# First stage of a graph network kernel: transpositions between the halves of a chunk's matmuls, and receivers' places ahead of the receiver table

## The chip, the cores and the metric

The kernel runs on one core of a Trainium2 chip. The metric is the device time of one execution in microseconds (us). Three runs of the kernel before the change took 4166.1, 4173.35 and 4174.21 us (median 4173.35). The engines are named as the profile names them: PE is TensorE (matmuls; PEld its weight loads), DVE is VectorE, ACT is ScalarE, POOL is GpSimd, SP is the engine that mostly issues transfers.

## What is computed

One layer of message passing on a graph with 12,500 nodes of 64 features and 412,500 edges of 32 features, all float32, receivers sorted. The reference, cut to what matters:

```python
h = jnp.maximum(_layernorm(x, axis=-1), 0.0)
msg_in = jnp.concatenate([h[senders], h[receivers], edge_features], axis=-1)
messages = swish(msg_in @ W1 + b1) @ W2 + b2
att = softmax(swish(msg_in @ Wa1 + ba1) @ Wa2 + ba2, axis=0)     # over all edges
aggregated = segment_sum(messages * att, receivers)
upd = swish(concatenate([h, aggregated], -1) @ Wu1 + bu1) @ Wu2 + bu2
return x + upd
```

Since `msg_in @ W` is a sum of three products, the kernel multiplies the sender and receiver parts once per node instead of once per edge.

## The kernel before, in words

**First stage** (`gnn_kernel`, L145 to L267). The nodes are padded to 12,544, which is 128 partitions times 98 blocks (`NB`). They are worked in eight chunks of 8, 14, 14, 14, 14, 14, 12 and 8 blocks (`sizes`, L155). SP's queue loads the eight chunks of x (L163), then `src_sb`, `base_sb`, `dst_sb` and `base_p` (L165 to L170): the senders' numbers, the first receiver of each group of edges (twice), and the receivers' numbers. ACT's queue loads the weights in two halves (L112, L113). For each chunk:

- `squares` (L193): DVE makes row sums `total` (L198) and subtracts the mean into `xm` (L200); ACT squares that into `sq` (L203).
- `deviation` (L206): DVE sums the squares (L208), ACT takes the root (L209).
- `normal` (L211): DVE takes the reciprocal (L214) and makes `h`, the normalised and rectified features (L216).
- `senders` (L219): PE transposes two blocks at a time into PSUM tiles `pt` of up to eight blocks (L229, two such buffers); ACT copies them to `hT` (L231); PE multiplies with the sender weights into PSUM tiles `pn` of up to four blocks (L236, four buffers); ACT copies each to `ts` (L238, two buffers); SP's queue writes the finished chunk into the senders' table `ts_d` in DRAM (L239).

All of these stand in an order written out by hand: `pin` (`tc.keep_in_program_order`) keeps each engine's instructions in the order of the source. In turn i that order is `deviation(i)`, `senders(i - 1)`, `squares(i + 2)`, `normal(i)` (L245 to L251). So on ACT, a chunk's two `hT` copies and four `ts` copies stand in a row, and on PE its seven transposes and seven products.

After the last chunk comes the receivers' table (L253 to L264): for each chunk PE multiplies the kept `hT` with the receiver weights (L259, the same `pn` buffers), DVE adds the bias into `tr` (L261, two buffers), and ACT's queue writes it to `tr_d` (L263). ACT's queue then writes a zero tail and all of `hT` to DRAM (L265, L266), which the main stage reads back. Then `windows` (L176) makes the receivers' places on DVE: `dloc`, each edge's receiver relative to its group's first one (L178, L182), `bj` (L184) and `far` (L187, L188).

**Main stage** (`one_pass`). The edges are 403 groups of 1024. `load(g)` has POOL issue eight indirect DMAs per group (L382), each fetching 128 rows of 512 B of `ts_d` by the numbers in `src_sb`, into one of eight `gs` buffers; SP's queue loads the edge features `eo` and receivers `db` of four groups at a time (L391, L394) and a 64-row window of `tr_d` (L401); DVE makes a one-hot block in `eo` (L405) and PE multiplies (L409). `begin(g)` adds both on DVE (L414) and takes tanh on ACT (L415); `end(g)` makes messages and logits on DVE (L425 to L436); `by_node` weighs and sums by receiver (L477, L483). A running maximum makes the softmax one pass. The tile framework hands eight semaphores in turn to POOL's gathers, so each gather waits until the one eight before it has landed; the transfers of SP and ACT share eight others in the same way. A last stage divides by the softmax sum and computes the update.

Of the kernel before, what the change touches and what calls it, by code (L numbers as in the profile page):

```python
# [42 lines left out]
F32 = mybir.dt.float32  # L43
I32 = mybir.dt.int32
AF = mybir.ActivationFunctionType
# [6 lines left out]
P = 128  # L52
D = 64
DE = 32
U = 64
C = 2 * U
# [24 lines left out]
def gnn_kernel(ctx: ExitStack, tc: tile.TileContext, n_edges, x, src, dst, dst_row, first, edge,  # L81
               weights, out):
    nc = tc.nc
    NB = x.shape[0] // P
# [3 lines left out]
    CB = 14 if NB % 14 == 0 else 2  # L88
# [5 lines left out]
    ts_d = dram.tile([NP, C], F32, name="ts_d")  # L94
# [11 lines left out]
    w_all = const.tile([P, sum(n for _, n in PARTS)], F32, name="w_all")  # L106
# [2 lines left out]
        part[name] = w_all[:, at:at + n]  # L109
        at += n  # L110
    nh = sum(n for _, n in PARTS[:HALVED])
    nc.scalar.dma_start(w_all[:, :nh], weights[:, :nh])  # L112
    nc.scalar.dma_start(w_all[:, nh:], weights[:, nh:])  # L113
    w_pair = part["pair"].rearrange("p (r n) -> p r n", r=2)
    wu2h = part["wu2h"].rearrange("p (h d) -> p h d", h=2)
    we, bias, wa2, bu2_r, ba2_c = (part[k] for k in ("we", "bias", "wa2", "bu2", "ba2"))
# [36 lines left out]
    with tc.tile_pool(name="node1", bufs=1) as node1, \  # L153
            tc.tile_pool(name="node", bufs=2) as node, \
            tc.tile_pool(name="node_ps", bufs=2, space=PSUM) as node_ps:  # L155
        x_v = x.rearrange("(p b) d -> p b d", b=NB)

        sizes = [8] + [min(CB, NB - 16 - c) for c in range(0, NB - 16, CB)] + [8] if NB > 16 else [NB]
        chunks = [(sum(sizes[:i]), n) for i, n in enumerate(sizes)]
        xcs = []  # L160
        for c, n in chunks:
            xc = node.tile([P, CB, D], F32, name="xc", bufs=min(len(chunks), 8))[:, :n, :]
            nc.sync.dma_start(xc, x_v[:, c:c + n, :])  # L163
            xcs.append(xc)
        nc.sync.dma_start(src_sb, src)  # L165
        nc.sync.dma_start(base_sb[:, :NG], first)
        dst_sb = node1.tile([P, T], I32, name="dst_sb")
        nc.sync.dma_start(dst_sb, dst)
        base_p = node1.tile([P, NG], I32, name="base_p")
        nc.sync.dma_start(base_p, bass.AP(tensor=first.tensor, offset=first.offset,  # L170
                                          ap=[[0, P], [1, NG]]))
        hT = node1.tile([2 * D, NB // 2, P], F32, name="hT")

        pin = tc.keep_in_program_order

        def windows():  # L176

            pin(nc.vector.tensor_tensor(dloc.rearrange("p (g k) -> p g k", k=K),  # L178
                                        dst_sb.rearrange("p (g k) -> p g k", k=K),
                                        base_p[:, :, None].to_broadcast([P, NG, K]), ALU.subtract))  # L180
            last4 = dloc.rearrange("p (g k) -> p g k", k=K)[:, :, H:]
            pin(nc.vector.tensor_scalar(last4, last4, -float(SHIFT), None, op0=ALU.add))  # L182
            for h in range(2):
                pin(nc.vector.tensor_scalar(bj[:, :, h], base_p[:WR, :], iota_p[:WR], float(SHIFT * h),  # L184
                                            op0=ALU.add, op1=ALU.add))
            fall = node1.tile([P, NG - 1], F32, name="fall")
            pin(nc.vector.tensor_tensor(fall, base_p[:, :NG - 1], base_p[:, 1:], ALU.subtract))  # L187
            pin(nc.vector.tensor_reduce(far[:, 2:3], fall, AX.X, ALU.max))  # L188

        eps = node1.tile([P, 1], F32, name="eps")  # L190
        nc.vector.memset(eps, EPS)
        xms, sqs, rstds, hs = {}, {}, {}, {}

        def squares(i):

            n = chunks[i][1]
            total = node.tile([P, CB], F32, name="total")[:, :n]
            pin(nc.vector.tensor_reduce(total, xcs[i], AX.X, ALU.add))  # L198
            xm = xms[i] = node.tile([P, CB, D], F32, name="xm", bufs=3)[:, :n, :]
            pin(nc.vector.scalar_tensor_tensor(xm, total[:, :, None].to_broadcast([P, n, D]), -1.0 / D,  # L200
                                               xcs[i], op0=ALU.mult, op1=ALU.add))
            sq = sqs[i] = node.tile([P, CB, D], F32, name="sq", bufs=3)[:, :n, :]
            pin(nc.scalar.activation(sq, xm, AF.Square))  # L203

        def deviation(i):
            n = chunks[i][1]  # L206
            rstd = rstds[i] = node.tile([P, CB], F32, name="rstd")[:, :n]
            pin(nc.vector.tensor_reduce(rstd, sqs.pop(i), AX.X, ALU.add))  # L208
            pin(nc.scalar.activation(rstd, rstd, AF.Sqrt, bias=eps, scale=1.0 / D))  # L209

        def normal(i):  # L211
            n = chunks[i][1]
            rstd = rstds.pop(i)
            pin(nc.vector.reciprocal(rstd, rstd))  # L214
            h = hs[i] = node.tile([P, CB, D], F32, name="h")[:, :n, :]
            pin(nc.vector.scalar_tensor_tensor(h, xms.pop(i), 0.0,  # L216
                                               rstd[:, :, None].to_broadcast([P, n, D]),
                                               op0=ALU.max, op1=ALU.mult))

        def senders(i):  # L220
            c, nn = chunks[i]
            h = hs.pop(i)
            ts = node.tile([P, CB, C], F32, name="ts")[:, :nn, :]
            pts = []
            for b in range(0, nn, 8):
                n = min(8, nn - b)
                pt = node_ps.tile([P, 4, P], F32, name="pt")
                for k in range(n // 2):
                    pin(nc.tensor.transpose(pt[:, k, :], h[:, b + 2 * k:b + 2 * k + 2, :], ident))  # L229
                q = (c + b) // 2  # L230
                pin(nc.scalar.copy(hT[:, q:q + n // 2, :], pt[:, :n // 2, :]))  # L231
            for b in range(0, nn, 4):
                m = min(4, nn - b)
                pn = node_ps.tile([P, 4, C], F32, name="pn", bufs=4)
                for k in range(0, m, 2):
                    pin(nc.tensor.matmul(pn[:, k:k + 2, :], hT[:, (c + b + k) // 2, :],  # L236
                                         w_pair[:, 0], start=True, stop=True))
                pin(nc.scalar.copy(ts[:, b:b + m, :], pn[:, :m, :]))  # L238
            pin(nc.sync.dma_start(ts_d.rearrange("(p b) f -> p b f", b=NB)[:, c:c + nn, :], ts))  # L239

        squares(0)
        if len(chunks) > 1:
            squares(1)
        pin(nc.vector.tensor_scalar(w_all[:, :nh], w_all[:, :nh], 0.5, None, op0=ALU.mult))
        for i in range(len(chunks)):  # L245
            deviation(i)
            if i:
                senders(i - 1)
            if i + 2 < len(chunks):
                squares(i + 2)  # L250
            normal(i)  # L251
        senders(len(chunks) - 1)
        for c, nn in chunks:  # L253
            tr = node.tile([P, CB, C], F32, name="tr")[:, :nn, :]
            for b in range(0, nn, 4):
                n = min(4, nn - b)
                pn = node_ps.tile([P, 4, C], F32, name="pn", bufs=4)
                for i in range(0, n, 2):
                    pin(nc.tensor.matmul(pn[:, i:i + 2, :], hT[:, (c + b + i) // 2, :],  # L259
                                         w_pair[:, 1], start=True, stop=True))  # L260
                pin(nc.vector.tensor_tensor(tr[:, b:b + n, :], pn[:, :n, :],  # L261
                                            bias[:, None, :].to_broadcast([P, n, C]), ALU.add))
            pin(nc.scalar.dma_start(  # L263
                tr_d[:NP, :].rearrange("(p b) f -> p b f", b=NB)[:, c:c + nn, :], tr))  # L264
        pin(nc.scalar.dma_start(tr_d[NP:, :], zero[:WR, :]))  # L265
        pin(nc.scalar.dma_start(hT_d, hT))  # L266
        windows()  # L267

    one_pass(tc, n_edges, locals())
    again = nc.values_load(wrong[0:1, 0:1], min_val=0, max_val=1,  # L270
# [615 lines left out]
```

## Time and profile before

One execution was profiled.

| what | value |
|---|---|
| median of three runs | 4173.35 us |
| time of the profiled execution | 4166.68 us |
| its span, first to last instruction | 4164.9 us |
| DVE busy | 2873.2 us (69%) |
| POOL busy | 3052.8 us (73%) |
| PE busy | 2237.8 us (54%) |
| ACT busy | 600.9 us (14%) |
| first gather starts | 56.44 us |
| last gather starts | 4091.0 us |
| DVE, ACT busy from 0 to 56.4 us | 34.96, 30.91 us |

A row of the page's fifth part names the source line, the engine and operation, the tile written and the tiles read, shapes and count; then the busy time and the mean ns of one; then the idle time just before such instructions and what ended most of it. "issue" there means that the engine waited for nothing that the profile shows. A row of the timeline gives the start, the duration, the engine, the line and the tiles; in brackets stands the idle time before it and what released it. Equal instructions that follow closely are merged into one row with their count. A float32 product counts as two matmul records. Queues are marked by a q: SPq and ACTq rows are the issuing of transfers, not the transfers.

### The profile page before, as it was taken

Reading aid. Unit: us, or ns where it says so; the run is one execution under the profiler, and the core shown is the slowest. Engines: PE = TensorE matmul, PEld = TensorE weight load, DVE = VectorE, ACT = ScalarE, POOL = GpSimd, SP = SyncE. Lnnn points to the kernel's source line nnn. Section 1 sums busy time; section 2 is a strip of 40 time slices with the busy share of each in tenths; the row PEclk is TensorE's granted clock in tenths of the full one; section 3 lists DMA queues with packets and bytes.
Section 4 is the critical chain, followed back from the end, with each engine's and each line's share of the span. In section 5 each row is a group of like instructions: output and inputs, shape, how many; then the busy total and the mean of one; then the engine's idle time right before and its main releaser. Section 6 shows DMA issues by size and latency. Waiting matters only on the chain.

```text
span 4164.9 us, 43769 instructions
## 1 busy us (share of the span) xinstructions
PE 2237.8 (54%) x10980; PEld 1678.3 (40%) x10980; DVE 2873.2 (69%) x7698; ACT 600.9 (14%) x1230; POOL 3052.8 (73%) x3236
## 2 busy tenths in 40 slices
PE   5544555545545555555555455555555555555555
PEld 4433434333434343443444334343344443444444
DVE  5867767766677676666766667666676666666668
ACT  2211111111111111111111111111111111111112
POOL 3777777777777777777777777777777777777772
PEclk8666666666666666666656655666565666656665
DMA  7433433333333333333333332333323333333323
GB/s 269 103 92 95 102 100 96 101 95 101 101 89 90 89 81 90 82 88 90 80 90 83 87 89 80 90 82 87 90 80 89 83 88 90 80 90 85 85 77 111
DMA packets 230871, 392.46 MB, mean 94 GB/s; under 512 B 97745, under 2 KB 156370, under 8 KB 217426
## 3 DMA queue, kind: packets, MB, share of 16 engines
q0 software_dynamic: 103168, 211.49, 19.1%
q1 hardware_dynamic: 125778, 167.76, 15.2%
q10 hardware_dynamic: 1664, 10.32, 0.6%
q8 instruction: 91, 1.49, 0.1%
q14 instruction: 170, 1.39, 0.1%
HBM read 363.56 MB, written 25.72 MB: 93 GB/s over the span
## 4 chain that ended last, share of the span: by engine, by line


## 5 line engine op out<-in xcount | busy, mean ns | idle before, releaser
L382 POOL DMA_INDIRECT gs<-ts_d,src_sb x3224 | 3051.2, 946 | 1038.3 <-issue 930.2
L409 PE MATMUL pe<-wins,eo 128*128 128x256 f32 x3224 | 1395.8, 608 | 1178.2 <-issue 1122.1
L409 PEld LDWEIGHTS pe<-wins,eo 128*128 128x128 f32 x3224 | 953.6, 310 | 1453.1 <-issue 1189.0
L414 DVE TENSOR_TENSOR gs<-pe,gs 128x1024 f32<-128x1024 f32 x403 | 491.8, 1220 | 1116.6 <-DMA gs<-ts_d,src_sb 1103.8
L415 ACT ACTIVATE pe<-gs 128x1024 f32<-128x1024 f32 x403 | 415.7, 1031 | 2760.5 <-DVE gs L414 2267.5
L477 DVE TENSOR_SCALAR wt<-iota_w,dloc,p 128x40 f32<-128x40 f32 x3224 | 725.2, 316 | 0.1
L483 PE MATMUL sp<-wt,acts 128*65 128x40 f32 x6448 | 586.0, 261 | 0.9 <-DVE wt L477 0.9
L483 PEld LDWEIGHTS sp<-wt,acts 128*65 128x65 f32 x6448 | 535.3, 173 | 26.7 <-DVE wt L477 1.0
L453 PE MATMUL mt<-ident,mx 128*128 128x128 f32 x103 | 48.6, 472 | 530.3 <-DVE sums L507 526.9
L425 DVE SCALAR_TENSOR_TENSOR acts<-pe,gs 128x512 f32<-128x512 f32 x403 | 271.9, 675 | 27.7 <-ACT pe L415 27.6
L433 DVE TENSOR_TENSOR pe<-pe,w_all 128x512 f32<-128x512 f32 x403 | 281.4, 698 | 12.8
L431 DVE SCALAR_TENSOR_TENSOR pe<-pe,gs 128x512 f32<-128x512 f32 x403 | 280.4, 696 | 11.2
L436 DVE TENSOR_REDUCE lg<-pe 128x8 f32<-128x512 f32 x403 | 276.9, 687 | 10.3
L405 DVE TENSOR_SCALAR eo<-db,bj 64x256 f32<-64x256 int32 x806 | 270.3, 373 | 8.0 <-DMA db<-in_dst_row_dram 0.4
L494 PEld LDWEIGHTS mt<-ss,w2u 65*64 65x64 f32 x806 | 99.2, 175 | 392.6 <-issue 378.6
L453 PEld LDWEIGHTS mt<-ident,mx 128*128 128x128 f32 x103 | 18.8, 182 | 543.1 <-DVE sums L507 538.9
L494 PE MATMUL mt<-ss,w2u 65*64 65x40 f32 x806 | 149.9, 280 | 160.5 <-DVE gm L460 148.0
L464 ACT ACTIVATE scale<-fall 128x1 f32<-128x1 f32 x103 | 20.9, 203 | 510.2 <-DVE fall L463 510.2
L508 DVE COPY sums<-nmax 64x40 f32 x403 | 79.1, 196 | 9.0 <-issue 0.2
L489 ACT COPY ss<-sp 65x40 f32<-65x40 f32 x403 | 73.5, 182 | 28.6 <-PE sp L483 28.6
L507 DVE TENSOR_TENSOR sums<-sums,mt 64x40 f32 x300 | 53.6, 179 | 3.5 <-PE mt L494 2.4
L290 ACT COPY bu<-mt 64x512 f32<-64x512 f32 x24 | 25.9, 1078 | 149.1 <-PE mt L287 149.1
(89 smaller groups left out, 591.3 us busy)
## 6 DMA issues: line engine op xcount, KB each, us to landing
gs<-ts_d,src_sb POOLq DMA_INDIRECT x3224
eo<-in_edge_dram SPq DMA_DIRECT2D x100, 512.0 KB
db<-in_dst_row_dram SPq DMA_DIRECT2D x200, 256.0 KB
wins<-tr_d SPq DMA_DIRECT2D x806, 32.0 KB
ts_d<-ts SPq DMA_DIRECT2D x5, 896.0 KB
tr_d<-tr ACTq DMA_DIRECT2D x5, 896.0 KB
hT_d<-hT ACTq DMA_DIRECT2D x1, 3136.0 KB
hb<-in_x_dram SPq DMA_DIRECT2D x24, 128.0 KB
```

Source lines behind the costliest of these rows:

```text
L382: nc.gpsimd.indirect_dma_start(out=gs[:, j, :], out_offset=None, in_=ts_d[:, :], in_offset=bass.IndirectOffsetOnAxis(ap=src_sb[:, t + j:t ...
L405: pin(nc.vector.tensor_scalar(eo[:WR, e], db[:, e], bj[:, g, h:h + 1], None, op0=ALU.is_equal))
L409: pin(nc.tensor.matmul(pe[:, 2 * q:2 * q + 2, :], eo[:, q * P:(q + 1) * P], win[:, q // 2, :, :], start=True, stop=True))
L414: pin(nc.vector.tensor_tensor(gss[g], pes[g], gss[g], ALU.add))
L415: pin(nc.scalar.activation(pes[g], gss[g], AF.Tanh))
L425: pin(nc.vector.scalar_tensor_tensor(acts[g % ACTS][:, :, 0:U], th[:, :, U:C], 1.0, gs[:, :, U:C], op0=ALU.add, op1=ALU.mult))
L431: pin(nc.vector.scalar_tensor_tensor(att, th[:, :, 0:U], 1.0, gs[:, :, 0:U], op0=ALU.add, op1=ALU.mult))
L433: pin(nc.vector.tensor_tensor(att, att, wa2[:, None, :].to_broadcast([P, K, U]), ALU.mult))
L436: pin(nc.vector.tensor_reduce(lgs[s][:, k:k + K], att, AX.X, ALU.add))
L477: pin(nc.vector.tensor_scalar(wt[:, j, :], iota_w[:, j // H, :], dloc[:, g * K + j:g * K + j + 1], p[:, k + j:k + j + 1], op0=ALU.is_equal ...
L483: pin(nc.tensor.matmul(sp, acts[g % ACTS][:, j, :], wt[:, j, :], start=j == 0, stop=j == K - 1))
L494: pin(nc.tensor.matmul(pp, w2u, sps.pop(g), start=True, stop=True))
```

## The change

Four things change, all in the first stage.

- The two loads of the weights move from ACT's queue to SP's, behind the second chunk of x.
- A root of one column (`spare`) is taken on ACT ahead of everything else there.
- `senders` is cut into `transpose` (transposes and `hT` copies) and `senders(i, first, last)` (products and `ts` copies of blocks `first` to `last`). In turn i the order is now: sum of squares of chunk i; transposes and `hT` copies of chunk i - 1; root of chunk i; products and `ts` copies of the blocks from 8 on of chunk i - 2, and that chunk's write to `ts_d`; row sum and subtraction of chunk i + 2; products and `ts` copies of the first eight blocks of chunk i - 1; square of chunk i + 2; reciprocal and `h` of chunk i. One turn is added at the end.
- `windows()` is called ahead of the receivers' table instead of after it.

The order of POOL's instructions is the same as before, and so is that of the main stage but for two one-row memsets on DVE and a few issues of `db` on SP's queue.

```diff
-    nc.scalar.dma_start(w_all[:, :nh], weights[:, :nh])
-    nc.scalar.dma_start(w_all[:, nh:], weights[:, nh:])
...
             nc.sync.dma_start(xc, x_v[:, c:c + n, :])
             xcs.append(xc)
+            if c == chunks[min(1, len(chunks) - 1)][0]:
+                nc.sync.dma_start(w_all[:, :nh], weights[:, :nh])
+                nc.sync.dma_start(w_all[:, nh:], weights[:, nh:])
...
+        pin(nc.scalar.activation(node1.tile([P, 1], F32, name="spare"), eps, AF.Sqrt))
...
-        def senders(i):
+        def transpose(i):
             c, nn = chunks[i]
             h = hs.pop(i)
-            ts = node.tile([P, CB, C], F32, name="ts")[:, :nn, :]
             pts = []
             for b in range(0, nn, 8):
                 n = min(8, nn - b)
                 pt = node_ps.tile([P, 4, P], F32, name="pt")
                 for k in range(n // 2):
                     pin(nc.tensor.transpose(pt[:, k, :], h[:, b + 2 * k:b + 2 * k + 2, :], ident))
                 q = (c + b) // 2
                 pin(nc.scalar.copy(hT[:, q:q + n // 2, :], pt[:, :n // 2, :]))
-            for b in range(0, nn, 4):
-                m = min(4, nn - b)
+
+        def senders(i, first, last):
+
+            c, nn = chunks[i]
+            last = min(last, nn)
+            if first == 0:
+                tss[i] = node.tile([P, CB, C], F32, name="ts")[:, :nn, :]
+            ts = tss[i]
+            for b in range(first, last, 4):
+                m = min(4, last - b)
                 pn = node_ps.tile([P, 4, C], F32, name="pn", bufs=4)
...
                 pin(nc.scalar.copy(ts[:, b:b + m, :], pn[:, :m, :]))
-            pin(nc.sync.dma_start(ts_d.rearrange("(p b) f -> p b f", b=NB)[:, c:c + nn, :], ts))
+            if last == nn:
+                pin(nc.sync.dma_start(
+                    ts_d.rearrange("(p b) f -> p b f", b=NB)[:, c:c + nn, :], tss.pop(i)))
...
-        for i in range(len(chunks)):
-            deviation(i)
-            if i:
-                senders(i - 1)
-            if i + 2 < len(chunks):
-                squares(i + 2)
-            normal(i)
-        senders(len(chunks) - 1)
+        for i in range(nch + 1):
+            if i < nch:
+                totals(i)
+            if i >= 1:
+                transpose(i - 1)
+            if i < nch:
+                deviation(i)
+            if i >= 2 and chunks[i - 2][1] > 8:
+                senders(i - 2, 8, CB)
+            if i + 2 < nch:
+                subtract(i + 2)
+            if i >= 1:
+                senders(i - 1, 0, 8 if i < nch else CB)
+            if i + 2 < nch:
+                square(i + 2)
+            if i < nch:
+                normal(i)
+        windows()
         for c, nn in chunks:
...
         pin(nc.scalar.dma_start(hT_d, hT))
-        windows()
```

`squares` is likewise cut into `subtract` (row sum, subtraction) and `square`, and `deviation` into `totals` (sum of squares) and `deviation` (root); `squares(0)` and `squares(1)` still stand ahead of the loop.

More of the change, by code (lines that the diff above doesn't have):

```diff
@@ L191, in gnn_kernel, with subtract @@
         nc.vector.memset(eps, EPS)
-        xms, sqs, rstds, hs = {}, {}, {}, {}
+        pin(nc.scalar.activation(node1.tile([P, 1], F32, name="spare"), eps, AF.Sqrt))
+        xms, sqs, rstds, hs, tss = ({} for _ in range(5))
         def squares(i):
+            subtract(i)
+            square(i)
+        def subtract(i):
             n = chunks[i][1]
@@ L201, in squares, with square, totals @@
                                                xcs[i], op0=ALU.mult, op1=ALU.add))
+        def square(i):
+            n = chunks[i][1]
             sq = sqs[i] = node.tile([P, CB, D], F32, name="sq", bufs=3)[:, :n, :]
-            pin(nc.scalar.activation(sq, xm, AF.Square))
-        def deviation(i):
+            pin(nc.scalar.activation(sq, xms[i], AF.Square))
+        def totals(i):
             n = chunks[i][1]
@@ L208, in deviation @@
             pin(nc.vector.tensor_reduce(rstd, sqs.pop(i), AX.X, ALU.add))
-            pin(nc.scalar.activation(rstd, rstd, AF.Sqrt, bias=eps, scale=1.0 / D))
+        def deviation(i):
+            pin(nc.scalar.activation(rstds[i], rstds[i], AF.Sqrt, bias=eps, scale=1.0 / D))
         def normal(i):
@@ L238, in senders @@
                 pin(nc.scalar.copy(ts[:, b:b + m, :], pn[:, :m, :]))
-            pin(nc.sync.dma_start(ts_d.rearrange("(p b) f -> p b f", b=NB)[:, c:c + nn, :], ts))
+            if last == nn:
+                pin(nc.sync.dma_start(
+                    ts_d.rearrange("(p b) f -> p b f", b=NB)[:, c:c + nn, :], tss.pop(i)))
+        nch = len(chunks)
         squares(0)
-        if len(chunks) > 1:
+        if nch > 1:
             squares(1)
         pin(nc.vector.tensor_scalar(w_all[:, :nh], w_all[:, :nh], 0.5, None, op0=ALU.mult))
-        for i in range(len(chunks)):
-            deviation(i)
-            if i:
-                senders(i - 1)
-            if i + 2 < len(chunks):
-                squares(i + 2)
-            normal(i)
-        senders(len(chunks) - 1)
+        for i in range(nch + 1):
[16 more added lines that the diff above has]
+        windows()
         for c, nn in chunks:
```

## The prediction

> **What bounds the kernel now.** I read the page's costliest groups, then the timeline of the first 140 us, last the waits of GpSimd (POOL). On the page:
>
> ```profile
> L382 POOL DMA_INDIRECT gs<-ts_d,src_sb x3224 | 3051.2, 946 | 1038.3 <-issue 930.2
> ...
> L414 DVE TENSOR_TENSOR gs<-pe,gs 128x1024 f32<-128x1024 f32 x403 | 491.8, 1220 | 1116.6 <-DMA gs<-ts_d,src_sb 1103.8
> ```
>
> POOL issues 3224 gathers of sender rows, and VectorE (DVE) waits 1103.8 us for what they fetch.  A gather takes 0.94 us and the next one starts 0.30 us later, so one gather costs about 1.249 us, and 3224 of them about 4027 us. They run from 56.44 to 4091.9 us; the 73 us after that are the last groups and the update stage. So the span is the start of the first gather, plus the gathers, plus a tail that this change doesn't touch. Only what moves the first gather, or what makes a gather slower, counts. The end of the first stage in the timeline:
>
> ```profile
> 46.11 2.46 PEld L236 LDWEIGHTS pn<-w_all,hT 128*128 128x128 f32 x12 [0.78 <-ACT hT L231]
> ...
> 49.48 0.59 ACT L231 COPY hT<-pt 128x512 f32<-128x512 f32 x1
> ...
> 52.16 0.58 ACT L238 COPY ts<-pn 128x512 f32<-128x512 f32 x1 [0.23 <-PE pn L236]
> 53.02 0.69 DVE L261 TENSOR_TENSOR tr<-pn,w_all 128x512 f32<-128x512 f32 x1 [6.41 <-PE pn L259]
> ...
> 56.44 1.10 POOL L382 DMA_INDIRECT gs<-ts_d,src_sb  x1 [54.04 <-issue]
> ```
>
> The last copy into ts ends at 52.74, the table's last write is issued, and 3.70 us after that copy the first gather starts. DVE has nothing to do for 6.41 us there. One chunk of the loop before that, in the same timeline:
>
> ```profile
> 29.73 0.96 ACT L203 ACTIVATE sq<-xm 128x896 f32<-128x896 f32 x1
> 30.58 0.30 ACT L209 ACTIVATE rstd<-rstd,eps 128x14 f32<-128x14 f32 x1
> 30.78 0.96 ACT L231 COPY hT<-pt 128x512 f32<-128x512 f32 x2
> 30.92 0.24 DVE L214 RECIPROCAL rstd<-rstd 128x14 f32<-128x14 f32 x1 [1.04 <-ACT rstd L209]
> 31.41 3.29 PE L236 MATMUL pn<-w_all,hT 128*128 128x256 f32 x14 [1.27 <-ACT hT L231]
> 32.62 0.58 ACT L238 COPY ts<-pn 128x512 f32<-128x512 f32 x1 [0.89 <-ACT hT L231]
> ```
>
> TensorE (PE) waits 1.27 us for ScalarE's (ACT's) copy of the transposes, ACT waits 0.89 us for PE's first product, and DVE waits 1.04 us for the root. A ring of three engines, none of them full. The chunks start 5.3 us apart here (reciprocals at 25.59, 30.92, 36.13). One more view, POOL's own timeline:
>
> ```profile
> 76.58 0.94 POOL L382 DMA_INDIRECT gs<-ts_d,src_sb  x1 [0.30 <-issue]
> 77.83 3.36 POOL L382 DMA_INDIRECT gs<-ts_d,src_sb  x1 [0.30 <-issue]
> 81.49 1.32 POOL L382 DMA_INDIRECT gs<-ts_d,src_sb  x1 [0.30 <-issue]
> ...
> 93.20 0.94 POOL L382 DMA_INDIRECT gs<-ts_d,src_sb  x1 [0.40 <-DMA gs<-ts_d,src_sb]
> 95.82 0.94 POOL L382 DMA_INDIRECT gs<-ts_d,src_sb  x1 [1.67 <-DMA gs<-ts_d,src_sb]
> ```
>
> Two gathers are stretched by 2.42 and 0.38 us while DVE works at the receivers' places (L178 runs from 76.86 to 80.36, L182 from 80.98 to 82.01). Four later ones wait for earlier gathers, 2.0 us over the usual 0.30 in all. Together 4.8 us of the gather stream are lost near its start. Nowhere else is more than some tenths lost at once.
>
> **What the skill says.** "SBUF — State Buffer", section "Who interferes with whom": a VectorE instruction with two SBUF inputs takes a read port that GpSimd shares, and the later of the two blocks until the other ends. The trace agrees: L178 has two SBUF inputs, and the stretched gather ends at 81.19, 0.83 us after L178. "ScalarE: Activation LUTs", section "Table sets: the hidden batching unit": functions are loaded by set. The trace has loads of 1.28 us at 1.75 and 9.84, and no further one among the squares and roots that alternate after the second. "DMA: Bandwidth & Descriptors", section "Issuing engines are not separate DMA queues": DMAs of all issuers share the same 16 engines. The trace agrees: while hT_d is written (80 to 85 us) 7 packets of gathers move, against 120 in the 5 us before.
>
> **The start.** The weights leave ACT's queue and stand on SP's behind the first two x chunks. Before, weights and x0 move together from 3 to 5 us and DVE starts at 4.82, then waits 0.40 for x1. Alone, x0 could be in about 0.7 us sooner: I take 4.1, with 4.82 (no gain) and 3.8 as ends. The 0.40 goes as well. SP's two issues (0.42 and 0.45 on ACT's queue) stand ahead of x2 to x7, src, base, dst and base_p. x2 is needed 4.7 us after x0. At the 0.41 MB/us of the trace, the 1.83 MB up to x2 are in by about 7.7 us, so that is hidden. The halving of the weights on DVE, which every later DVE step stands behind, needs them 3.5 us after x0, at 7.6; they land by about 6.3. Later, it would cost one for one, at most 2 us. The second table load at 9.84 disappears; DVE reaches the reciprocal that follows only at 12.01, behind its own work, so it is worth nothing. The spare root costs 0.3 us of an idle ACT. Gain at the root of chunk 1: 1.1 us.
>
> **The loop.** Per chunk of 14 the old and new order have the same work. DVE's back-to-back starts give 1.00 (total of squares) + 1.11 (row sum) + 1.01 (subtraction) + 0.34 (reciprocal) + 1.01 (h) = 4.47 us; chunk 1 to chunk 2 took just 4.40 before the ring formed (L208 at 12.84 and 17.24). PE: 7 transposes 0.93, 7 products at 0.43, together 3.94. ACT: 0.86 + 0.20 + 0.76 + 0.86 + 0.85 = 3.5, about 4 with its waits. In the new order PE has the three last products of the former chunk to run while ACT copies the transposes, so its 1.27 us of waiting are filled. ACT places the hT copies ahead of the root. They may start 0.68 us after the transposes do, the root follows 0.96 later, and DVE needs the root only after its row sum and subtraction, 3.1 us after h. That leaves some 0.5 us of slack, so DVE should not wait in the middle of the loop. Behind these copies on ACT are queued the root, four ts copies and the square, which is needed two chunks later. The first turn is worse: PE is slow there (two products take 1.7 us), ACT does the square of chunk 3 first, and the root of chunk 2 then ends near 20.0 where DVE would take it at 19.2. So 0.8 of the 1.1 us are given back, and the total of chunk 3 starts at 21.4 instead of 21.70.
>
> From there I lay the new order out engine by engine with these durations. The totals (L208) of chunks 4, 5, 6, 7 start at 25.9, 30.1, 34.1, 38.0, against 26.95, 32.27, 37.49, 42.34. That is 4.5, 4.2, 4.0 and 3.9 us per turn (the shorter ones hold the chunks of 12 and 8) against 5.25, 5.32, 5.22 and 4.85: 4.0 us saved, after 0.3 at the head.
>
> **The end of the stage.** After the last total, at 38.0: hT copies of chunk 6 from 39.0 to 39.8, root, reciprocal at 40.2, h from 40.5 to 41.2. PE meanwhile finishes chunk 5 and half of chunk 6 at 42.0, transposes chunk 7 to 42.55, does the rest of chunk 6 to 43.4, then four products of chunk 7 from 43.5 to 45.2. The last copy ends at 46.1. From last total to last copy this is 8.1 us against 10.4. So 0.3 + 4.0 + 2.3 = 6.6 us. ts has two buffers, and the wait for the write of two chunks ago now stands one turn nearer: a write lands about 3.6 us after its issue and is needed 4.9 us after it, hidden by 1.3 us. The last two writes overlap now (1.3 MB from 45.2 at 0.41 MB/us end by 48.5), in time for the same 3.7 us. First gather: 49.8 instead of 56.44. Ends: 4.5 us of gain (x no sooner, a wait at each root), 8 us (x at 3.8 and no loss at chunk 2).
>
> **The receivers' places.** 3.50 + 1.03 + 0.74 + 0.56 + 0.57 with gaps are 6.7 us on DVE, now from 41.2 to 47.9, in the idle stretch that the old trace shows as 6.41. dst_sb and base_p are in by 22 us (the load queue is empty from there). Behind them waits the receiver table on DVE (L261); its first product is ready near 46.2, so it is held 1.7 us. PE fills its four PSUM buffers and stops, and DVE catches up at 0.57 a block against PE's 0.87. The table's writes and hT_d then go some 6.2 us earlier than before. They are not on the path of the gathers: eight groups of gather buffers last POOL until some 80 us after its start, and the first group is freed at 113 us, 57 after. Without that cover each microsecond would count.
>
> **What the gathers win.** All of the places are done before the first gather, so the 2.8 us of stretching go. But the waits come next: each gather waits for the eighth one before it, and hT_d's write keeps those from landing. Before, gather 32 starts at 100.10 where an undisturbed stream would have it at 95.3. After, POOL is two gathers further when hT_d starts (24.0 us after the first gather, 23.6 before), nearly all of them still on their way. So most of the 2.8 us turns into waiting. I take 0.7 us of gain; ends 0 and 4.8.
>
> Sum: 6.6 + 0.7 = 7.3 us. The profiled execution took 4166.68 (span 4164.9 and 1.8 around it), so 4159.4 for its like. The runs shown are 4166.1, 4173.35 and 4174.21, median 4173.35: that less 7.3 is 4166.0. With the profiled one there are two low runs (about 4166.4) and two high ones, whose middle is 4170.0; less 7.3 that is 4162.7. I say 4164, between the two, which puts the base at 4171.3. 0.2% is 8.35 us, about what a measurement can tell from no change; the old kernel's runs alone spread over 8 us.
>
> **Rivals.** (A) The queue of eight doesn't bind: hT_d's write overlaps fewer gathers, and stretch and waits both vanish. Then 6.6 + 4.8 = 11.4, so 4160. For it: the waits came to only 2.0 us before. Against: POOL arrives there with more gathers on their way. (B) The ring stays: a root behind the hT copies reaches DVE later than the subtraction in every turn, so that turns last about 5.0; only head, tail and some 0.3 us a turn remain, 3.5 us, so 4168. For it: slack of only 0.5 us. Against: ACT's sum of 3.5 to 4 us is below DVE's 4.47. (C) Slower: the same mechanism further on. If transposes, copies, root, products and their copies follow one another with no overlap, DVE is held from the reciprocal on. It decides once the root ends over 1.35 us (0.5 slack, 0.85 gain) later than laid out; 3 us later costs 1.65 more on each of six turns, 10 us, less 2.6 for head and tail: 4179. Against: the pt buffers (two) and pn buffers (four) let PE run ahead. (D) The change doesn't reorder what it says: the compiled queues show it as described, so I give it nothing.
>
> **Chances.** Forecast 0.55, A 0.2, B 0.17, C 0.08. Range: from A off the low runs (4166.4 - 11.4 = 4155) to B off the high ones (4174.2 - 3.5 = 4171); the forecast's ends lie inside. Faster by over 0.2%: 0.45 of the forecast, most of A, little of B, 0.42; slower 0.07, most of C; within 0.2%: 0.51.
>
> **What would show it.** First gather at about 49.8; totals 4.0 to 4.5 us apart; no gather over 1.2 us before 100 us; gather 32 at about 93 with 3 to 5 us of waits for earlier gathers; last gather 7 us sooner and the 73 us tail unchanged. Wrong if DVE's reciprocals show waits for the root in the middle turns, if ts copies wait for a DMA, or if the stream's rate of 1.249 us moves, which times 3224 outweighs all of this.

## The result, and the profile after

| | before | after |
|---|---|---|
| median of 18 runs each | 4173.31 us | 4165.03 us |
| lowest and highest run | 4166.1, 4174.76 | 4156.93, 4168.67 |
| profiled execution, and its span | 4166.68, 4164.9 | 4156.93, 4155.2 |
| first gather starts | 56.44 | 51.98 |
| gather 32 (counted from 1) starts | 100.10 | 92.94 |
| stretched gathers, over 0.94 us each | 2.80 us in all (two gathers) | none |
| waits for earlier gathers, over the usual 0.30 us | 2.02 us | 2.13 us |
| last gather starts | 4091.0 | 4082.0 |
| from there to the end of the span | 73.9 | 73.2 |

The ratio is 0.998, with a 95% interval of 0.9973 to 0.9986: 8.3 us less, between 5.8 and 11.3. The forecast was 7.3 us. The profiled executions lie 6.6 and 8.1 us under the median of their kernel, so they are compared with each other only. In the last four runs below every kernel, the one before too (5472.5 us), took some 1300 us longer, with waits of up to 10.5 us of VectorE for TensorE's products from about 60 us on, so of their traces only what comes up to the first gather is read.

The page of the kernel after has the same two costliest groups as before. The rate of the stream has not moved: 3224 gathers of 945 ns, where it was 946.

```profile
L412 POOL DMA_INDIRECT gs<-ts_d,src_sb x3224 | 3046.6, 945 | 1033.9 <-issue 933.7
...
L444 DVE TENSOR_TENSOR gs<-pe,gs 128x1024 f32<-128x1024 f32 x403 | 491.7, 1220 | 1107.0 <-DMA gs<-ts_d,src_sb 1088.1
```

One turn of the loop, in the timeline of the kernel after:

```profile
27.07 0.96 ACT L212 ACTIVATE sq<-xm 128x896 f32<-128x896 f32 x1
...
27.83 3.19 PE L254 MATMUL pn<-w_all,hT 128*128 128x256 f32 x14
27.93 0.95 ACT L241 COPY hT<-pt 128x512 f32<-128x512 f32 x2
28.76 0.33 ACT L220 ACTIVATE rstd<-rstd,eps 128x14 f32<-128x14 f32 x1
...
28.97 0.87 ACT L256 COPY ts<-pn 128x512 f32<-128x512 f32 x2
29.66 0.23 DVE L225 RECIPROCAL rstd<-rstd 128x14 f32<-128x14 f32 x1
```

None of these rows has a bracket: the waits of 1.27, 0.89 and 1.04 us that PE, ACT and DVE had here are gone. PE's fourteen matmul records run through, the root ends at 29.09 and DVE comes to the reciprocal at 29.66, 0.57 later. The end of the stage, in the same timeline:

```profile
41.57 3.51 DVE L179 TENSOR_TENSOR dloc<-dst_sb,base_p 128x3224 f32<-128x3224 int32 x1
...
47.19 1.07 ACT L256 COPY ts<-pn 128x512 f32<-128x512 f32 x2 [2.50 <-DMA ts_d<-ts]
47.30 0.57 DVE L189 TENSOR_REDUCE far<-fall 128x1 f32<-128x402 f32 x1
47.79 1.90 DVE L292 TENSOR_TENSOR tr<-pn,w_all 128x512 f32<-128x512 f32 x3
...
51.98 1.10 POOL L412 DMA_INDIRECT gs<-ts_d,src_sb  x1 [49.58 <-issue]
```

The places fill DVE from 41.57 to 47.87 and the receiver table starts right behind them, 5.2 us sooner than before. But the last copies into `ts` have a new wait: 2.50 us for the write of two chunks ago. SP's queue issued that write (chunk 5, 0.92 MB) at 41.53:

```profile
41.53 0.32 SPq L258 DMA_DIRECT2D ts_d<-ts  x1
...
48.29 0.32 SPq L258 DMA_DIRECT2D ts_d<-ts  x1
```

The copy could start at 47.19, so the write landed 5.7 us after its issue (the expectations below say 5.6). The second row is the last write; the first gather follows it by 3.7 us. POOL's own timeline after that:

```profile
85.83 0.95 POOL L412 DMA_INDIRECT gs<-ts_d,src_sb  x1 [1.54 <-DMA gs<-ts_d,src_sb]
...
91.14 0.94 POOL L412 DMA_INDIRECT gs<-ts_d,src_sb  x1 [0.63 <-DMA gs<-ts_d,src_sb]
92.94 0.94 POOL L412 DMA_INDIRECT gs<-ts_d,src_sb  x1 [0.86 <-DMA gs<-ts_d,src_sb]
```

No gather is stretched, and the waits for earlier gathers are much as before (2.13 us for 2.02). Of the 9.0 us at the last gather, 4.5 come from the first stage, 2.7 more are there by gather 32, and 1.8 come along the rest of the stream. The last part is not the change's: from gather 32 to the last one the ten profiled executions of ordinary length took between 3989 and 3995 us, without order among the kernels.

So the sum was near and two of its terms were not. The first gather moved by 4.5 us instead of 6.6; the gathers up to the 32nd gave 2.7 instead of 0.7. On the new wait two theories stand against each other: the places, now on DVE beside that write, hold it up; or a write of this size simply takes so long. On the stretch, too: the queue of eight takes most of it back and the 2.7 us have another source; or it is a gain by itself. The experiments bear on both.

### The profile page after: what moved, and what is told of

The parts are those of the page before. It is cut to its first block, busy times and chain, and to the rows that moved or that the text cites. A ratio compares the mean times of both kernels' runs of the same rounds, so it can differ in the third digit from the quotient of the medians.

```text
span 4155.2 us, 43768 instructions
## 1 busy us (share of the span) xinstructions
PE 2243.6 (54%) x10980; PEld 1682.4 (40%) x10980; DVE 2874.9 (69%) x7698; ACT 599.4 (14%) x1230; POOL 3048.2 (73%) x3236
## 4 chain that ended last, share of the span: by engine, by line
```

## The experiments

Each block of rows ran on one chip, in turn with the kernel before (median in brackets). The columns: median, ratio to the kernel before with its interval, start of the first gather and of gather 32 in the profiled execution.

| run | median us | ratio | first | 32nd |
|---|---|---|---|---|
| b_windows_early (4166.83) | 4163.5 | 0.9992 [0.9984, 1.0] | 56.38 | 96.71 |
| a_windows_late | 4161.33 | 0.9987 [0.998, 0.9993] | 50.79 | 95.17 |
| a_ts3 | 4156.71 | 0.9975 [0.9966, 0.9985] | 50.77 | 91.83 |
| a_weights_act | 4158.49 | 0.998 [0.9972, 0.9988] | 52.12 | 93.24 |
| after_again (4165.98) | 4157.1 | 0.9979 [0.9971, 0.9987] | 50.32 | 91.33 |
| a_root_first | 4156.93 | 0.9979 [0.9971, 0.9987] | 50.96 | 92.39 |
| a_hT_pieces | 4155.15 | 0.9973 [0.9963, 0.9984] | 50.0 | 88.91 |
| a_ts3_halves | 4155.65 | 0.9974 [0.9965, 0.9984] | 50.16 | 90.9 |
| f_order_only (5472.52) | 5467.84 | 0.9997 [0.9983, 1.0011] | 50.6 | not read |
| a_ts3_pieces | 5465.21 | 0.9982 [0.9968, 0.9995] | 50.11 | not read |
| f_ts3_pieces_root | 5473.36 | 1.0 [0.9985, 1.0016] | 49.51 | not read |
| f_all | 5475.48 | 1.0008 [0.9996, 1.002] | 50.73 | not read |

**The places alone.** b_windows_early is the kernel before with one line moved; a_windows_late is the kernel after with it moved back.

```diff
         senders(len(chunks) - 1)
+        windows()
         for c, nn in chunks:
...
         pin(nc.scalar.dma_start(hT_d, hT))
-        windows()
```

> The kernel before with one edit: the receivers' places are made ahead of the receivers' table. Theory 1 (the queue of eight takes back what the stretched gathers win): first gather unchanged near 56.4 us, no gather above 1.2 us, waits for earlier gathers near hT_d's write grow from 2.0 to 4 us or more, gather 32 starts at 99 to 100.1, time 0 to 1 us under before. Theory 2 (the stretch is a plain loss): waits stay at 2 us, gather 32 starts at 97.3, time 2.8 us under before.

> The changed kernel with the receivers' places put back behind the receivers' table. It tells why the write of chunk 5 of ts landed 5.6 us after its issue and held ScalarE for 2.5 us. Theory 1 (VectorE's 3.5 us instruction on the places slows the write that runs beside it): the wait of ScalarE for the ts buffer is under 0.5 us, first gather near 49.8. Theory 2 (a write takes that long whenever the next one follows it closely): the wait stays near 2.5 us, first gather near 52. In both the stretched gathers return; time 1 us over or under the changed kernel.

In b_windows_early the first gather stays (56.38), the stretch is gone, and gather 32 starts 3.4 us sooner; the median is 3.3 us lower (interval 0 to 6.7). The queue did not take it back. POOL's timeline there has 1.78 us of waits, the last 0.31 of them just behind gather 32, where the kernel before had 2.02:

```profile
91.57 0.94 POOL L382 DMA_INDIRECT gs<-ts_d,src_sb  x1 [1.62 <-DMA gs<-ts_d,src_sb]
...
96.71 0.94 POOL L382 DMA_INDIRECT gs<-ts_d,src_sb  x1 [0.45 <-DMA gs<-ts_d,src_sb]
98.27 0.94 POOL L382 DMA_INDIRECT gs<-ts_d,src_sb  x1 [0.61 <-DMA gs<-ts_d,src_sb]
```

With the places late again, the new first stage alone leaves 5.5 us, and a gather is stretched even more than before, by 3.54 us. POOL's rows and DVE's, of a_windows_late:

```profile
72.17 4.48 POOL L412 DMA_INDIRECT gs<-ts_d,src_sb  x1 [0.30 <-issue]
```

```profile
72.00 3.50 DVE L179 TENSOR_TENSOR dloc<-dst_sb,base_p 128x3224 f32<-128x3224 int32 x1
```

The gather starts 0.17 us after the DVE instruction with two SBUF inputs and ends 1.15 us after it. This is what the Trainium skill says in "SBUF — State Buffer", section "Who interferes with whom": the later of the two blocks until the earlier one ends. The same section also tells of a probe in which a `tensor_tensor`, the kind of DVE's instruction here, did not stall DMA; these gathers were held up, and here the measurement decides. What it costs depends on where a gather falls: 2.42 us in the kernel before, 3.54 here. The two parts agree with the whole: 3.3 for the places and 5.5 for the rest (2.9 to 8.3) make 8.8, and the whole change made 8.9 in after_again, on another chip. With intervals of some 3 us either way this is no proof that they add exactly.

The same run answers for the new wait on `ts`. No DVE instruction of the places runs there before 72 us, and still ACT waits for two writes:

```profile
42.01 1.07 ACT L256 COPY ts<-pn 128x512 f32<-128x512 f32 x2 [1.03 <-DMA ts_d<-ts]
...
45.98 1.08 ACT L256 COPY ts<-pn 128x512 f32<-128x512 f32 x2 [1.82 <-DMA ts_d<-ts]
```

The second is for the write of chunk 5 again, issued at 41.00 and landed by 45.98: 5.0 us. after_again, with the places on DVE from 40.61, has it at 5.0 as well (issued 40.57, copy at 45.55). So the wait does not come from the places, though they may add some tenths. Nor does a write of 0.92 MB always take so long. That of chunk 5 took 5.7 us in the result, 5.6 in a_weights_act, 4.3 in a_root_first and 3.7 in f_order_only (41.86 to 45.52); that of chunk 3 took 5.9 in a_root_first (33.16 to 39.07). Neither theory covers this spread, and its cause stays open. When the copy would have come without the wait is seen in a_ts3, the next run: 3.6 us after that issue (41.10 to 44.71). So a write of 3.7 us costs next to nothing there, and one of 5.0 to 5.7 us holds the copy by 1.4 to 2.1.

**A third buffer for ts.**

```diff
-                tss[i] = node.tile([P, CB, C], F32, name="ts")[:, :nn, :]
+                tss[i] = node.tile([P, CB, C], F32, name="ts", bufs=3)[:, :nn, :]
```

> The changed kernel with three ts buffers in place of two. The wait of ScalarE for the write of two chunks ago goes, so the first gather starts 2 to 2.5 us sooner, near 49.6. Theory 1 (from then on hT_d's write and the queue of eight set the pace, and the table waits for the places as before): waits of the gathers near hT_d's write grow by 1 to 2 us, gather 32 near 92, time 0.5 to 1.5 us under the changed kernel. Theory 2 (only the first gather counts): gather 32 near 90.5, time 2.5 us under.

No copy waits for a write any more, and the last copy ends at 46.12, as the prediction laid out (46.1). But the first gather comes 4.65 us after it, not 3.7. From the last total (the sum of squares of the last chunk) to the first gather it is 12.53 us; with two buffers it is 12.62 in after_again and 13.31 in the result. So taking the wait away won next to nothing against after_again. The last two writes are issued 1.85 us apart there (44.29 and 46.14), for 2.90 in after_again, and it would fit that the last one stands behind the other on the same engines. But in f_order_only and f_ts3_pieces_root, further down, they are 1.86 us apart, and the first gather still comes 3.7 us after the last copy. What makes it 4.65 stays open.

**The weights back on ACT's queue.**

```diff
+    nc.scalar.dma_start(w_all[:, :nh], weights[:, :nh])
+    nc.scalar.dma_start(w_all[:, nh:], weights[:, nh:])
...
-            if c == chunks[min(1, len(chunks) - 1)][0]:
-                nc.sync.dma_start(w_all[:, :nh], weights[:, :nh])
-                nc.sync.dma_start(w_all[:, nh:], weights[:, nh:])
```

> The changed kernel with the weights back on ScalarE's queue, ahead of x. Theory 1 (what x wins at the start is lost again by waiting for the weights and for the third chunk of x): the sum of squares of chunk 1 starts within 0.3 us of the 12.71 of the changed kernel, first gather within 0.5 us of 51.98, time within 1 us. Theory 2 (the move is worth the 1.1 us of the forecast): first gather and time 1 us later.

The sum of squares of chunk 1 starts at 13.03 there. With the weights on SP's queue it starts between 11.61 (a_hT_pieces) and 12.71 (the result) in ten profiled executions, so the move gives between 0.3 and 1.4 us. What varies most is the weights' arrival. DVE's timeline of the result:

```profile
3.67 0.69 DVE L204 TENSOR_REDUCE total<-xc 128x8 f32<-128x512 f32 x1 [2.55 <-DMA xc<-in_x_dram]
...
8.09 0.63 DVE L265 TENSOR_SCALAR w_all<-w_all 128x896 f32<-128x896 f32 x1 [0.89 <-DMA w_all<-in_weights_dram]
...
9.75 1.09 DVE L204 TENSOR_REDUCE total<-xc 128x14 f32<-128x896 f32 x1 [0.43 <-DMA xc<-in_x_dram]
```

DVE starts 1.15 us sooner than before (3.67 for 4.82) and then loses 0.89 to the weights and 0.43 to x2. In after_again the weights are in time and only x2 is late, by 0.37. The medians of a_weights_act and of a_ts3 differ by 1.8 us, which the buffer and the weights share.

**The kernel after once more, and the root first.** after_again is the kernel after, unedited. a_root_first puts the root back ahead of the `hT` copies:

```diff
-            if i >= 1:
-                transpose(i - 1)
             if i < nch:
                 deviation(i)
+            if i >= 1:
+                transpose(i - 1)
```

> The changed kernel as it is, on the same chip as the next three. First gather 51.5 to 52.2 us, gather 32 at 92.6 to 93.4, ratio to the kernel before 0.998.

> The changed kernel with the root of a chunk put ahead of the transposes' copies on ScalarE, as it was before the change. Theory 1 (putting the copies first is worth little, since VectorE's 4.5 us of work bound the turns either way): turns of 4.2 to 4.5 us as in the changed kernel, VectorE's waits for the root at chunks 2, 6 and 7 (0.68, 1.68, 1.31 us) shrink, first gather within 1 us of the changed kernel, time within 1.5 us. Theory 2 (the copies' place is what opens the ring): turns go back towards 5 us, first gather and time 2 to 4 us later than the changed kernel.

In after_again the first gather came at 50.32, sooner than the 51.5 to 52.2 expected of it, because the weights were in time. With the root first, the turns from chunk 3 on do not change, 4.5 to 3.7 us in both orders: in the middle of the loop the copies-first order buys nothing, because both orders fit. At chunk 2 copies first costs: the reciprocal waits 0.68 us for the root in after_again and not at all with the root first, where the turn to chunk 3 takes 4.46 us for 5.24. At the last chunk it is the root first that costs. The last total comes at 36.62 there, 1.1 us sooner than in after_again, and then the `ts` copies that stand ahead of the root on ACT wait for a write. ACT's row, then DVE's:

```profile
39.07 1.07 ACT L256 COPY ts<-pn 128x512 f32<-128x512 f32 x2 [2.07 <-DMA ts_d<-ts]
```

```profile
40.37 0.20 DVE L225 RECIPROCAL rstd<-rstd 128x8 f32<-128x8 f32 x1 [3.07 <-ACT rstd L220]
```

The gain is gone at the reciprocal (40.37 for 39.70 in after_again); the medians are 0.2 us apart. What else in the new order does away with the waits of the loop was not tried part by part.

**hT in seven pieces.** The write of `hT` to DRAM, one transfer of 24.5 KB per partition, is cut:

```diff
-        pin(nc.scalar.dma_start(hT_d, hT))
+        for q in range(0, NB // 2, 7):
+            pin(nc.scalar.dma_start(hT_d[:, q:q + 7, :], hT[:, q:q + 7, :]))
```

> The changed kernel with the write of hT to DRAM cut into seven writes of 3.5 KB per partition instead of one of 24.5 KB; the bytes are the same. Theory 1 (the large packets of that write shut the gathers out, and the queue of eight turns this into waits of POOL): the waits of 2.1 us fall under 0.7, gather 32 starts 1.5 to 2 us sooner, time 1.5 to 2 us less. Theory 2 (the transfer engines are simply full, by bytes): waits and time as in the changed kernel, within 0.7 us.

No gather waits for an earlier one, and gather 32 starts 2.4 us sooner than in after_again. The bytes are the same, so it is not by them alone that the write made the gathers wait. Is it the size of the packets? The queues' packets and MB from 76 to 82 us, of the kernel after (q0 is POOL's gathers, q10 ACT's writes):

```profile
q10 hardware_dynamic: 80, 2.01, 89.7%
...
q0 software_dynamic: 63, 0.13, 5.4%
```

and from 74 to 76 us, of a_hT_pieces:

```profile
q10 hardware_dynamic: 204, 0.66, 102.4%
...
q0 software_dynamic: 4, 0.02, 2.2%
```

Packets of 25 KB let 63 gather packets of 2 KB through in 6 us. But packets of 3.2 KB, where they fill the engines, let through only 4 in 2 us. The gathers' packets in two stretches:

| run | 74 to 82 us | 82 to 90 us |
|---|---|---|
| after | 77 | 173 |
| after_again | 85 | 212 |
| a_hT_pieces | 88 | 346 |

Up to 82 us, while the whole write runs, the pieces help little. Their gain comes behind it, where the pieces (issued over 7.6 us) still move and SP's loads take a smaller share, 27% of the engines for 76% in after_again. So cutting the write took the waits away in this trace; whether by the size of the packets, by the gaps between the pieces or by when SP's loads come is not shown, and it was not tried on the kernel before. The time is 2.0 us under that of after_again on the same chip, but the intervals overlap: that it beats the kernel after is suggested by the trace up to gather 32 and not settled by the clock. It is the lowest median of all runs of ordinary length, and below the kernel before by 0.27% (0.16 to 0.37).

**Parts written as they are copied.** a_ts3_halves has three `ts` buffers, writes each part of `ts` when it is copied, and cuts the last chunk in two:

```diff
-            if last == nn:
-                pin(nc.sync.dma_start(
-                    ts_d.rearrange("(p b) f -> p b f", b=NB)[:, c:c + nn, :], tss.pop(i)))
+            pin(nc.sync.dma_start(
+                ts_d.rearrange("(p b) f -> p b f", b=NB)[:, c + first:c + last, :], ts[:, first:last, :]))
...
-                senders(i - 1, 0, 8 if i < nch else CB)
+                senders(i - 1, 0, 8 if i < nch else 4)
+                if i == nch:
+                    senders(i - 1, 4, CB)
```

> The changed kernel with three ts buffers, and each part of a chunk's table written as soon as it is copied (the last chunk in two parts) instead of the whole chunk at its end. With three buffers alone the last copy ended at 46.12 but the first gather started 4.65 us later instead of 3.70, as the last two writes shared the transfer engines. Theory 1 (those bytes waited for the end of the chunk): the first gather follows the last copy by 3.2 to 3.7 us, at 49.2 to 49.8, gather 32 at 90.5 to 91, time 2.5 to 3.5 us under the changed kernel. Theory 2 (the engines are full from 42 us on, whatever the order): first gather at 50.5 to 51 as with three buffers alone, time 1.5 to 2 us under.

The end is shorter: 11.26 us from last total to first gather (38.90 to 50.16) against 12.53 with the third buffer alone. The first turns are longer: the root of chunk 3 is late, a wait that the kernel after does not have. DVE's row:

```profile
25.69 0.24 DVE L225 RECIPROCAL rstd<-rstd 128x14 f32<-128x14 f32 x1 [1.23 <-ACT rstd L220]
```

The first gather is 0.16 us sooner than in after_again, between what the two theories had, and the median 1.45 lower. The late root goes back to PE. Its first products for chunk 1, of a_ts3_halves and of a_ts3:

```profile
19.35 3.78 PE L254 MATMUL pn<-w_all,hT 128*128 128x256 f32 x8 [0.51 <-ACT hT L241]
```

```profile
19.98 1.99 PE L254 MATMUL pn<-w_all,hT 128*128 128x256 f32 x8 [0.51 <-ACT hT L241]
```

The same eight records take 1.8 us longer here, as long as those of chunk 0 take in the result (3.78 us). Why PE stays slow for a turn more is open; nothing says that the writes in parts do it.

**The order alone, and the parts together.** f_order_only keeps only the new order and the spare root (weights on ACT's queue, places late). a_ts3_pieces joins the third buffer and the pieces; f_ts3_pieces_root puts the root first as well; f_all adds parts written separately for the last two chunks:

```diff
-            if last == nn:
+            if i >= nch - 2 or last == nn:
+                b = first if i >= nch - 2 else 0
...
```

> Only the new order of the first stage: the weights on ScalarE's queue and the receivers' places behind the table, as before the change. If the order and the places are separate gains, as the runs so far say: turns of 3.8 to 4.5 us, first gather at 51 to 52 us (4.5 to 5.5 sooner than before the change), the stretched gathers back (2.5 to 3.7 us), gather 32 at 95.2 to 96, time 4 to 5 us under the kernel before. If the order only pays together with the places: time within 2 us of the kernel before.

> The changed kernel with three ts buffers and hT written in seven pieces. ScalarE's wait for the ts buffer and the gathers' waits are both gone; the first gather is then held by the last two writes of the table. If both gains add: first gather 49.5 to 50.3, gather 32 at 88.2 to 89.2, time 2.5 to 3.5 us under the changed kernel. If the write of ts was only a wait in place of the transfer engines' limit: as with the pieces alone, 2 us under.

> As the run before it, and with the root ahead of the copies on ScalarE. With the root first alone the last sum of squares started 1.1 us sooner, and then the last root stood 3.07 us behind ts copies that waited for a buffer. With three buffers that wait is gone, so if nothing else is late next: first gather 48.5 to 49.3, gather 32 at 87.2 to 88.2, time 1 us under the run before it. If the last writes to the table set the first gather anyway: no difference.

> As the run before it, and with the last two chunks of the table written in parts as they are copied. If the shared transfer of the last two writes (4.65 us from the last copy to the first gather with three buffers, 3.70 without overlap) is what is left: first gather 47.6 to 48.5, gather 32 at 86.3 to 87.3, time 0.5 to 1 us under the run before it, 4.5 to 5.5 us under the changed kernel. If the engines are full there whatever the order: no difference to the run before it.

The totals of these four decide nothing. Up to the first gather they agree with the rest. The order alone moves the first gather to 50.6, 5.8 us. Root first with three buffers gives the earliest of all, 49.51, where 48.5 to 49.3 was expected. f_all, expected at 47.6 to 48.5, is behind it at 50.73: the root of chunk 3 is late again (1.26 us), and again PE's eight records take 3.71 us there for 1.99 in f_ts3_pieces_root. No arrangement tried brought the first gather under 49.5. Whether the third buffer and the pieces add up in the time stays open.

## Why the prediction was right, and where its steps were not

**What bounds the kernel.** Right. The 1.249 us per gather and the tail stayed, and what the first gather and the gathers before 100 us gained is the gain: 3.4 us for the places alone, 3.3 in the time.

**The start.** The mechanism was right, and "that is hidden" was not. x0 came at 3.67, sooner than the 4.1 taken; x2 was 0.2 to 0.45 late in all ten executions; the weights, forecast for 6.3, were late in five of the ten, by 0.16 to 0.89 us (needed at 7.20 and there at 8.09 in the result). In the profiled execution the 1.1 us at chunk 1 shrank to 0.13; in after_again it was 1.09. The loss at chunk 2, laid out as a root 0.8 us late, measured 0.68.

**The loop.** Right to 0.2 us a turn. The totals of chunks 3 to 7 were forecast for 21.4, 25.9, 30.1, 34.1 and 38.0. The result has 22.35, 26.81, 31.00, 34.83 and 38.67, all of them late by what was lost at the start (the head); after_again, with its head as forecast, has 21.38, 25.85, 30.04, 33.87 and 37.70. No reciprocal waits for a root in the middle turns: the slack of 0.5 us was 0.57. Those of the last two chunks wait 1.68 and 1.31 us, about as laid out. Rivals B and C did not occur.

**The end of the stage.** Here a term failed: "a write lands about 3.6 us after its issue and is needed 4.9 us after it, hidden by 1.3 us". The 3.6 us were the time of the last write, of 0.52 MB; the one that is waited for has 0.92 MB and took 5.7 and 5.0 in the two executions of the kernel after. And at the end of the stage it is needed 3.6 us after its issue (a_ts3), not 4.9, so that even a write of 3.6 us would have had nothing to spare. The wait that followed is 2.5 us, or 1.0 and 1.8. Taking it away in a_ts3 won little, for the second half of the forecast failed there: with the last two writes close behind each other the first gather did not come "in time for the same 3.7 us" but 4.65 after the last copy (4.64 in a_ts3_pieces). In f_order_only and f_ts3_pieces_root that half held. From last total to first gather 11.8 us were forecast and 12.6 and 13.3 measured in the kernel after; f_order_only, with the shortest write, has 11.6. With the late head (0.7 us) and the late end (1.5 us), the first gather is 2.2 us behind the forecast 49.8; in after_again it is 0.5 behind.

**The receivers' places.** Right: 41.57 to 47.87 on DVE against 41.2 to 47.9, the table right behind them, and nothing of that on the gathers' path.

**What the gathers win.** The other term that failed: "most of the 2.8 us turns into waiting". Expected were 3 to 5 us of waits up to gather 32; they are 1.5 to 2.5 in the nine profiled executions of ordinary length that write hT_d in one piece, with the stretch or without. I had let the gathers land at the pace of the old trace. And POOL was not "two gathers further when hT_d starts": ACT issued that write 19.6 us after the first gather in the result (71.59) and 21.6 before (77.99). Counting POOL's packets (32 of 2 KB are a gather), gathers moved by 80, 86, 90, 94 and 98 us:

```
before           16.8  17.1  19.0  21.2  25.9
b_windows_early  16.7  18.4  20.4  23.2  28.9
after_again      18.1  22.0  25.4  30.8  35.1
a_hT_pieces      18.6  24.3  30.6  34.0  36.0
```

In the first two the first gather and hT_d's write come at nearly the same times. With no gather stretched, more of them get through beside the write: 56 packets for 9 from 80 to 86 us. That POOL then has more of them queued fits this, and nothing tried separates it from other readings. Either way the landing curve was not given. The forecast "0.7 us of gain; ends 0 and 4.8" became 2.7 in the result and 3.4 alone. Rival A was right in half: the stretch vanished, the waits stayed, and they needed another edit.

**The sum.** 4.5 + 2.7 = 7.2 us in the profiled pair by gather 32, for 6.6 + 0.7 = 7.3 forecast. Two errors of about 2 us with opposite signs hide behind that, so that it came so near is luck. The medians give 8.3, and 8.9 on the chip of after_again, where the head was as forecast. The 4164 was 1.0 us low: the kernel before had its median at 4173.3, where I took 4171.3, and the gain was 1.0 more.

## What to carry to other kernels

Time a wait for a transfer by a transfer of the same size, and from more than one execution: the last, small write said "hidden" of a larger one, and the larger one took from 3.7 to 5.9 us. Take the moment at which it is needed from the place where it is needed soonest, here the end of the stage and not the middle of the loop. When a stall is taken out of a stream, do not lay the old trace's landing times under the new stream. And look at the large writes that run beside many small transfers: cutting one into seven took away waits that neither kernel's order could.

## What the runs showed of the hardware

- Writes of 0.92 MB from SBUF to DRAM that a copy waited for landed 3.7 us (f_order_only, chunk 5) to 5.9 us (a_root_first, chunk 3) after their issue; in the kernel after that of chunk 5 took 5.7 and 5.0. From the issue of the last write, 0.52 MB, to the first gather it was 3.7 us in the kernel after and 4.6 in a_ts3.
- Beside packets of 25 KB, gathers moved 63 packets in 6 us (the kernel after, 76 to 82 us). Beside packets of 3.2 KB that filled the engines they moved 4 in 2 us (a_hT_pieces, 74 to 76 us).
- The same eight matmul records of chunk 1 took 1.99 us in a_ts3 and 3.78 in a_ts3_halves, at the same place in the stage.
- A DVE instruction of 3.5 us with two SBUF inputs stretched a gather on GpSimd from 0.94 to 3.36 and to 4.48 us: the gather that was issued while it ran, and it ended 0.83 and 1.15 us after that instruction.
- From gather 32 to the last gather, profiled executions of kernels with the same main stage scattered by 6 us of 3990. Differences of 2 us are to be read in the first 100 us of a trace, or in medians.
